# Attention's scratches split in two, its load pools opened with the prologue, and later layers' weights turned amid the prologue

## The chip, the cores and the metric

The kernel runs on one core of a Trainium2 chip, in one launch. The metric is the device time of one execution in microseconds, from runs without a profiler. A further execution was recorded by the hardware profiler; its times, counted from its first instruction, are those of the profile.

## The reference

The input is x (3327 tokens of 128 features) and a dense array adj (3327 by 3327, mostly zeros, but read in full). Four layers follow, each of the form layernorm(x + layer(x)). The first is an attention whose reshape makes it large:

```python
q = (x @ Wq.T).reshape(d, n, h)          # d = 128, n = 3327, h = 8
k = (x @ Wk.T).reshape(d, n, h)
v = (x @ Wv.T).reshape(d, n, h)
a = jnp.einsum('dnh,dmh->dnm', q, k) * scale
a = a + spatial_encoding + edge_encoding  # both are adj
a = jax.nn.softmax(a, axis=2)
out = jnp.einsum('dnm,dmh->dnh', a, v)
return out.reshape(n, h * d) @ Wo.T
```

So there are 128 "heads" of 3327 by 3327 scores over only 8 features each: 1.4 thousand million exponentials. Head d reads a flat stretch of the projected array, tokens 26 d to 26 d + 26 or so. The other three layers are products with adj or its transpose, with normalisations by its row or column sums, and small weights w1, w2 and w3.

## The kernel before

**Prologue** (the block with the pools pw, pa, ppw, pps). Tokens are taken in seven "supers" of 512 (the last has 255); `spread` says how they lie. At the start x of all supers is loaded (`xr`), transposed on TensorE and copied to `xT` (VectorE) and `xN` (ScalarE). The weights Wq, Wk and Wv are loaded and transposed by `load_by_h`. Then, for each super u:

- `split(u, wqT, q_s, ...)` multiplies 128 tokens at a time by Wq (`products`, two PSUM buffers pp), writes the high part `hi` on ScalarE and the rest `lo` on VectorE, reduces `hi` to a largest value (`top_q`) on VectorE, and stores both from GpSimd's queue to the DRAM scratch q_s (`store_slots`); `split` with Wk does the same for k_s. `hi` and `lo` have a tag of their own each, with two buffers.
- `values_projected(u)` makes `vp`, eight features of the values by 512 tokens.
- `values_turned(d)` turns the values of two heads on TensorE into `vo` (copied by VectorE and ScalarE in turn), for all heads whose tokens are there; after every 16 heads ScalarE issues four stores to the scratch v_img.
- For u from 1 to 4, 128 rows of adj are loaded (`ar`) and reduced to their largest values (`tops`). `ar` and `vo` share the tag "wide" of two buffers.

After the last super, the weights of later layers (w1, w3, Wo) are transposed and stored to DRAM, and a flag is computed that says whether queries and keys are small enough.

**Attention** (`attention`). Queries are taken in seven blocks of CW = 476 columns, keys in four blocks of 6 or 7 times 128, so there are 28 blocks. In each, 32 groups of four heads follow each other. `load_edges` loads a block of adj (`e_in`), which TensorE transposes into the PSUM of the scores. `load_heads` loads queries and keys of one group (`qt`, `kt`, 11 DMAs on SP's queue), two groups ahead; `load_values` loads a pair of groups' values (`vs`), which GpSimd copies into `v_pad`. `copy_queries` makes negated and copied rows of `qt` on VectorE. Then, per head, three sets of scores are multiplied, go through the exponential on ScalarE (one in 24 is computed on VectorE instead), and are multiplied by the values (`weigh`). Beside this, the background transposes adj to DRAM piece by piece (`piece_load` into `ai`, `piece_work`, `piece_store`).

**What sets the order.** In attention the order on TensorE, ScalarE, GpSimd and VectorE is written out by hand. SP's order, and all of the prologue, is laid out by a scheduler when the kernel is built. Each engine runs its instructions in order and waits at each for what it needs. Transfers signal eight semaphores for SP and ScalarE together and eight for GpSimd, in turn: a new transfer waits until the one eight before it has landed. A pool that lies on memory of a closed pool waits until all users of that are done. So the first loads of attention wait for the whole prologue.

Of the kernel before, what the change touches and what calls it, by code (L numbers as in the profile page):

```python
# [10 lines left out]
F32 = mybir.dt.float32  # L11
# [8 lines left out]
P = 128  # L20
GROUP = 4
# [29 lines left out]
def kernel(ctx: ExitStack, tc: tile.TileContext, x, adj, wq, wk, wv, wo,  # L51
# [62 lines left out]
    q_s = scratch.tile([2 * H, RS], F32, name="q_s")  # L114
    k_s = scratch.tile([2 * H, RS], F32, name="k_s")

    v_img = scratch.tile([P, T * HD], F32, name="v_img")
# [126 lines left out]

    with tc.tile_pool(name="pw", bufs=1) as pw, tc.tile_pool(name="pa", bufs=2) as pa, \
# [9 lines left out]
        xT = pw.tile([P, NU, 4, P], F32, name="xT")  # L255
        xN = pw.tile([P, NU * SUPER], F32, name="xN")
        wqT = load_by_h(pw, ppw, wq, "wqT")
        for u in range(NU):
            base, R, full, rest = spread(u)
            xr = pa.tile([P, 4, D], F32, name="xr")  # L260
# [11 lines left out]
            nc.vector.tensor_copy(xT[:, u, 0:R, :], ps[:, 0:R, :])  # L272
            nc.scalar.copy(xN[:, base:base + R * P].rearrange("c (p r) -> c r p", r=R), ps[:, 0:R, :])
            if u == 0:
                wkT = load_by_h(pw, ppw, wk, "wkT")
                wvT = load_by_h(pw, ppw, wv, "wvT")

        def store_slots(eng, dram, row, u, sb):

            base, R, full, rest = spread(u)  # L280
            width = dram.shape[1]
            for a, n, k in ([(0, P, R)] if full == P else [(0, 112, R), (112, full - 112, R), (full, 1, rest)]):
                eng.dma_start(out=flat_ap(dram, row * width + (base + R * a) * D, [[R * D, n], [width, H], [1, k * D]]),
                              in_=sb[a:a + n, :, 0:k, :].rearrange("p h r j -> p h (r j)"))

        def products(u, r, w):
            pp = pps.tile([P, HD], F32, tag="pp", name="pp")
            for c in range(0, HD, 512):
                nc.tensor.matmul(pp[:, c:c + 512], lhsT=xT[:, u, r, :], rhs=w[:, c:c + 512], start=True, stop=True)
# [13 lines left out]
        def values_projected(u):  # L303
            n = spread(u)[1] * P
            vp[u] = pa.tile([P, H, SUPER], F32, name="vp")
            for h in range(H):
                ps = pps.tile([P, SUPER], F32, tag="ps", bufs=3, name="pv")
                nc.tensor.matmul(ps[:, 0:n], lhsT=wvT[:, h * D:(h + 1) * D], rhs=xN[:, u * SUPER:u * SUPER + n],
# [3 lines left out]
        def values_turned(d):  # L312

            g, i = d // 16, d % 16
            if i == 0:
                vo[g] = pa.tile([P, 4, T, 32], F32, tag="wide", name="vo")
# [16 lines left out]
            if i == 14:  # L333
                for k0, nt in KBS:
                    w = nt * 32
                    nc.scalar.dma_start(out=flat_ap(v_img, k0 * HD + g * 4 * w, [[T * HD, P], [w, 4], [1, w]]),
                                        in_=vo[g][:, :, k0:k0 + nt, :].rearrange("p g s c -> p g (s c)"))

        def split(u, w, s, top, f):
            hi = pa.tile([P, H, 4, D], F32R, tag="hi", name="hi")  # L340
            lo = pa.tile([P, H, 4, D], F32R, tag="lo", name="lo")
# [15 lines left out]
        for u in range(NU):  # L357
            split(u, wqT, q_s, top_q, SCALE / 2)
# [6 lines left out]
            if 1 <= u <= 4:  # L365
                ar = pa.tile([P, NP], F32, tag="wide", name="ar")
                load_rows(nc.sync, ar[:, 0:N], adj, u - 1)
                nc.vector.tensor_reduce(tops[:, u - 1:u], ar[:, 0:N], AX.X, ALU.max)
            if u == 4:
                store_tops(pw, 0, tops, P)  # L370
        assert d == D

        w1T = load_transposed(pw, ppw, w1, "w1T")
        nc.gpsimd.dma_start(out=w1T_s, in_=w1T.rearrange("p a b -> p (a b)"))
        w3T = load_transposed(pw, ppw, w3, "w3T")
        nc.gpsimd.dma_start(out=w3T_s, in_=w3T.rearrange("p a b -> p (a b)"))

        wo_raw = pw.tile([P, HD], F32, tag="w_raw", name="wo_raw")
        nc.sync.dma_start(out=wo_raw, in_=wo)
        woT = pw.tile([P, HD], F32, name="woT")  # L380
        for h in range(H):
            ps = ppw.tile([P, P], F32, tag="w_ps", name="w_ps")
            nc.tensor.transpose(ps, wo_raw.rearrange("p (j h) -> p h j", h=H)[:, h, :], ident)
# [854 lines left out]
```

## Time and profile before

| what | us |
|---|---|
| median of 3 runs | 10949.95 (10942.28 to 10952.19) |
| the profiled execution's own time | 10954.31 |
| its span, first to last instruction | 10952.1 |
| ScalarE busy / TensorE busy in the span | 9867.2 / 10557.4 |
| first exponential of attention starts | 333.9 |
| last exponential starts | 10179.5 |

Busy TensorE is not TensorE at its peak, since matmuls overlap and their ends are modelled. In the profile L611 is the exponential, L603 the scores, L628 the product with the values, L596 the transposes of adj, L463 and L470 the loads of queries and keys, L437 and L439 those of e_in, L283 the stores of q_s and k_s, L289 the products of the prologue, L345 and L346 its hi and lo, L327 the turning of values and L336 their stores, L88 the load of ar.

### The profile page before, as it was taken

What the parts mean: (1) busy time and instruction counts of PE and PEld (TensorE: products, weight loads), DVE (VectorE), ACT (ScalarE), POOL (GpSimd) and SP (SyncE); (2) the same over time, 40 slices, a digit from 0 to 9 for tenths busy, and PEclk for the clock granted to TensorE, in tenths of its full rate; (3) what the DMA queues carried; (4) which work ended last, traced back from release to release, by engine and by line L of the source; (5) the groups of instructions that cost most, each with busy time, mean ns of one, the idle gap of its engine ahead of it and who ended that gap; (6) DMA issues with size and microseconds to landing.
All of it is one profiled execution on the core that took longest, in us unless ns stands there. A gap on an engine that the chain in (4) does not pass through costs nothing. (4 is left out here: it accounts for less than half of the span.)

```text
span 10952.1 us, 201583 instructions
## 1 busy us (share of the span) xinstructions
PE 10557.4 (96%) x76941; PEld 4117.7 (38%) x76941; DVE 7291.7 (67%) x8351; ACT 9867.2 (90%) x10783; POOL 1585.4 (14%) x2742
## 2 busy tenths in 40 slices
PE   8899999999999999999999999999999999999999
PEld 5333333333333333333333333333333333333779
DVE  6566776667776677766777667776677766667412
ACT  3799999999999999999999999999999999999400
POOL 0111122111221111211112111121111100001200
PEclk9899999999999999999999999999999999999999
DMA  7988888888888888888888888888888888888676
GB/s 251 155 127 122 128 133 132 127 123 129 134 132 128 123 127 132 135 123 127 128 132 134 120 122 120 123 132 125 127 127 123 120 119 116 115 112 117 207 284 244
DMA packets 995053, 1516.11 MB, mean 138 GB/s; under 512 B 202471, under 2 KB 812577, under 8 KB 980267
## 3 DMA queue, kind: packets, MB, share of 16 engines
q1 hardware_dynamic: 896854, 1371.75, 78.7%
q0 software_dynamic: 79616, 116.88, 4.6%
q8 instruction: 623, 10.21, 0.5%
q10 hardware_dynamic: 17620, 14.49, 0.4%
q14 instruction: 340, 2.79, 0.1%
HBM read 1371.86 MB, written 130.35 MB: 137 GB/s over the span
## 5 line engine op out<-in xcount | busy, mean ns | idle before, releaser
L611 ACT ACTIVATE e<-sc 128x952 f32<-128x952 f32 (+1 forms) x10304 | 9644.5, 1067 | 227.8 <-PE sc L603 219.9
L628 PE MATMUL o<-e,v_pad 128*32 128x476 f32 (+1 forms) x46592 | 5639.9, 573 | 39.9 <-DVE acc L641 36.7
L603 PE MATMUL sc<-qt,kt 64*128 64x476 f32 x23296 | 4474.9, 438 | 252.6 <-ACT e L611 167.3
L603 PEld LDWEIGHTS sc<-qt,kt 64*128 64x128 f32 x23296 | 2187.6, 184 | 4561.8 <-ACT e L611 4254.8
L628 PEld LDWEIGHTS o<-e,v_pad 128*32 128x32 f32 (+1 forms) x46592 | 1039.9, 108 | 1942.4 <-issue 1898.4
L509 POOL COPY v_pad<-vs 128x192 f32<-128x192 f32 (+1 forms) x896 | 441.6, 519 | 8127.9 <-DMA vs<-v_img 6389.5
L567 DVE TENSOR_SCALAR ey<-sc 128x952 f32<-128x952 f32 x448 | 515.0, 1150 | 1631.8 <-PE sc L603 1631.2
L573 DVE SCALAR_TENSOR_TENSOR e<-e,ey 128x952 f32<-128x952 f32 x1344 | 1546.0, 1150 | 43.2
L493 DVE TENSOR_SCALAR qt<-qt 32x1428 fp32r<-32x1428 f32 x896 | 801.8, 895 | 428.9 <-DMA qt<-q_s 347.7
L495 DVE CAST qt<-qt 64x1904 fp32r<-64x1904 f32 x896 | 1035.1, 1155 | 30.5
L234 POOL DMA_DIRECT2D adjT_s<-at x1352 | 796.2, 596 | 185.4 <-DMA adjT_s<-at 130.8
L569 DVE SCALAR_TENSOR_TENSOR ey<-et,ey 128x952 f32<-128x952 f32 x448 | 516.5, 1153 | 15.5
L573 DVE SCALAR_TENSOR_TENSOR e<-e,et 128x952 f32<-128x952 f32 x448 | 514.7, 1149 | 12.5
L573 DVE SCALAR_TENSOR_TENSOR e<-ey 128x952 f32<-128x952 f32 x448 | 515.2, 1150 | 0.0
L1074 PE MATMUL bank<-y,eT 128*128 128x128 f32 (+1 forms) x4056 | 473.9, 276 | 0.4 <-DVE h L1196 0.4
L1074 PEld LDWEIGHTS bank<-y,eT 128*128 128x128 f32 (+1 forms) x4056 | 465.3, 192 | 5.7 <-DVE h L1196 0.6
L641 DVE TENSOR_TENSOR acc<-o,acc 128x476 f32<-128x476 f32 x231 | 150.2, 650 | 422.6 <-PE o L628 422.0
L494 DVE TENSOR_SCALAR qt<-qt 32x476 fp32r<-32x476 f32 x896 | 357.0, 398 | 7.6 <-DMA qt<-lead_s 5.9
L568 DVE TENSOR_SCALAR et<-ey 128x952 f32<-128x952 f32 x448 | 296.9, 663 | 15.4
L570 DVE TENSOR_SCALAR et<-et 128x952 int32<-128x952 int32 x448 | 295.0, 659 | 15.4
L1034 ACT ACTIVATE rstd<-mv,eps 128x1 f32<-128x1 f32 x104 | 30.4, 292 | 265.1 <-DVE mv L1032 265.1
L648 POOL DMA_DIRECT2D o_s<-acc x308 | 191.5, 626 | 35.8 <-DVE acc L641 22.4
(152 smaller groups left out, 2404.6 us busy)
## 6 DMA issues: line engine op xcount, KB each, us to landing
kt<-k_s SPq DMA_DIRECT2D x5320, 96.0 KB
kt<-k_s SPq DMA_DIRECT2D x1764, 128.0 KB
eT<-adjT_s SPq DMA_DIRECT2D x78, 1664.0 KB
qt<-q_s SPq DMA_DIRECT2D x896, 119.0 KB
qt<-q_s SPq DMA_DIRECT2D x1792, 59.5 KB
vs<-v_img SPq DMA_DIRECT2D x224, 224.0 KB
adjT_s<-at POOLq DMA_DIRECT2D x1352, 32.0 KB, 5.2
vs<-v_img SPq DMA_DIRECT2D x224, 192.0 KB
```

Of the source, the lines that this page charges most:

```text
L234: nc.gpsimd.dma_start(out=flat_ap(adjT_s, (t * P + 32 * q) * NP + c * PIECE, [[NP, 32], [P, ns], [1, P]]), in_=at[32 * i:32 * i + 32].rear ...
L493: return [(0.9, None, lambda: nc.vector.tensor_scalar(qt[32:64, 1:], qf[0:32, 0:GROUP - 1], -1.0, None, ALU.mult)), (0.4, None, lambda: nc ...
L494: (0.4, None, lambda: nc.vector.tensor_scalar(qt[32:64, 0], before, -1.0, None, ALU.mult)),
L495: (1.2, None, lambda: nc.vector.tensor_copy(qt[64:128], qf[0:64]))]
L509: nc.gpsimd.tensor_copy(vp[:, 32:32 + nt * GROUP * 32].rearrange("p (x c) -> p x c", c=32)[:, :, 0:H], vs.rearrange("p (x c) -> p x c", c=H))
L567: nc.vector.tensor_scalar(y, x, -58 * math.log(2.0), 2 / math.log(2.0), ALU.max, ALU.mult)
L569: vec.append((1.2, of, lambda: nc.vector.scalar_tensor_tensor(y, t, ROUND, y, ALU.subtract, ALU.subtract)))
L573: vec.append((1.2, of, lambda i=i, a=a: nc.vector.scalar_tensor_tensor(e, e if i else y, a, t if i == len(POLY) - 1 else y, ALU.add, ALU.m ...
L603: nc.tensor.matmul(s[:, i, 0:CW], lhsT=kt[64 * rg:64 * rg + 64, k, pos * P:(pos + 1) * P], rhs=qt[64 * rg:64 * rg + 64, k, :], start=False ...
L611: nc.scalar.activation(e[:, 0:n, :], s[:, 0:n, 0:CW], AF.Exp, scale=2.0)
L628: nc.tensor.matmul(o[32 * j:32 * j + 32, 0:CW], lhsT=values[b, g][:m, c:c + 32], rhs=es[b, g * GROUP + j, r][:m, :], start=(r == 0 and u = ...
L1074: nc.tensor.matmul(ps[:n, 0:D], lhsT=e[:m, s, :n], rhs=y[:m, s, col:col + D], start=(s == 0), stop=(s == T - 1))
```

## The change

- q_s, k_s and v_img become two DRAM scratches each. Groups from LATE = 29 on (values: from VLATE = 28) read the second one, all others the first, to which the last super writes nothing. Tokens of super 5 that both need are stored to both.
- The pools kq (kt, qt, vs) and ed (e_in) are opened before the prologue's pools and stay open through attention.
- To make room, x is transposed super by super (`tokens_turned`) into double-buffered xT and xN; hi, lo and ar share a tag of three buffers; vo has a tag of its own and half the size, so v_img is stored after every 8 heads.
- The weights w1, w3 and Wo are turned after super 3 and no longer after the last.

In the order as built, SP issues e_in and the leading row of the keys at the start, the loads of groups 0, 1 and 2 between the loads of x and ar, and reads the flag among the first loads of attention. The last product with Wk (super 6) stands on ScalarE behind the last stores of v_img.

```diff
-    q_s = scratch.tile([2 * H, RS], F32, name="q_s")
-    k_s = scratch.tile([2 * H, RS], F32, name="k_s")
-    v_img = scratch.tile([P, T * HD], F32, name="v_img")
+    q_s = [scratch.tile([2 * H, RS], F32, name=f"q_s{i}") for i in range(2)]
+    k_s = [scratch.tile([2 * H, RS], F32, name=f"k_s{i}") for i in range(2)]
+    v_img = [scratch.tile([P, T * HD], F32, name=f"v_img{i}") for i in range(2)]
+    LATE, VLATE = 29, 28
...
+    early = ctx.enter_context(ExitStack())
+    kq = early.enter_context(tc.tile_pool(name="kq", bufs=3))
+    ed = early.enter_context(tc.tile_pool(name="ed", bufs=1))
...
-        for u in range(NU):
+        def tokens_turned(u):
             base, R, full, rest = spread(u)
+            xTs[u] = pa.tile([P, 4, P], F32, name="xT")
+            xNs[u] = pa.tile([P, SUPER], F32, name="xN")
             xr = pa.tile([P, 4, D], F32, name="xr")
...
-            for a, n, k in ([(0, P, R)] if full == P else [(0, 112, R), (112, full - 112, R), (full, 1, rest)]):
-                eng.dma_start(out=flat_ap(dram, row * width + (base + R * a) * D, [[R * D, n], [width, H], [1, k * D]]),
+            late = max(0, ((LATE * GROUP - 1) * N // D - base) // R)
+            parts = [(0, P, R)] if full == P else [(0, 112, R), (112, full - 112, R), (full, 1, rest)]
+            pieces = [(0, *x) for x in parts] if u < NU - 1 else []
+            pieces += [(1, *x) for x in parts] if late == 0 else [(1, late, P - late, R)] if late < P else []
+            for i, a, n, k in pieces:
+                eng.dma_start(out=flat_ap(dram[i], row * RS + (base + R * a) * D, [[R * D, n], [RS, H], [1, k * D]]),
...
-            g, i = d // 16, d % 16
+            g, i = d // 8, d % 8
             if i == 0:
-                vo[g] = pa.tile([P, 4, T, 32], F32, tag="wide", name="vo")
+                vo[g] = pa.tile([P, 2, T, 32], F32, name="vo")
...
-            hi = pa.tile([P, H, 4, D], F32R, tag="hi", name="hi")
-            lo = pa.tile([P, H, 4, D], F32R, tag="lo", name="lo")
+            hi = pa.tile([P, H, 4, D], F32R, tag="hl", bufs=3, name="hi")
+            lo = pa.tile([P, H, 4, D], F32R, tag="hl", bufs=3, name="lo")
...
+            if u:
+                tokens_turned(u)
             split(u, wqT, q_s, top_q, SCALE / 2)
...
-                ar = pa.tile([P, NP], F32, tag="wide", name="ar")
+                ar = pa.tile([P, H, 4, D], F32, tag="hl", bufs=3, name="ar").rearrange("p h r j -> p (h r j)")
...
+            if u == 3:
+                w1T = load_transposed(pw, ppw, w1, "w1T")
+                nc.gpsimd.dma_start(out=w1T_s, in_=w1T.rearrange("p a b -> p (a b)"))
+                w3T = load_transposed(pw, ppw, w3, "w3T")
...
+                nc.gpsimd.dma_start(out=woT_s, in_=woT)
             if u == 4:
                 store_tops(pw, 0, tops, P)
...
-        with tc.tile_pool(name="acc", bufs=1) as accp, tc.tile_pool(name="kq", bufs=3) as kq, \
-                tc.tile_pool(name="ed", bufs=1) as ed, tc.tile_pool(name="ex", bufs=1) as ex, \
+        with tc.tile_pool(name="acc", bufs=1) as accp, tc.tile_pool(name="ex", bufs=1) as ex, \
...
-                                      in_=flat_ap(q_s, a * RS + c0 + d * N, [[RS, n], [N, GROUP], [1, CW]]))
+                                      in_=flat_ap(q_s[g >= LATE], a * RS + c0 + d * N, [[RS, n], [N, GROUP], [1, CW]]))
...
     attention()
+    early.close()
```

The loads of kt and vs choose their scratch in the same way as that of qt. In the changed kernel the exponential is L629, hi and lo are L361 and L362, the stores of q_s and k_s L298, those of v_img L351.

## The prediction

> **What bounds the kernel now.** I read the page first. Its costliest group is the exponential on ScalarE:
>
> ```profile
> L611 ACT ACTIVATE e<-sc 128x952 f32<-128x952 f32 (+1 forms) x10304 | 9644.5, 1067 | 227.8 <-PE sc L603 219.9
> ```
>
> 9644.5 us of a 10952.1 us span go to it, so attention is bound by ScalarE. I then compared the built orders: from the first transposes of scores on, TensorE, VectorE, ScalarE and GpSimd run the same instructions in the same order in both kernels (only the three steps that set the flag move in among VectorE's first ones). So 9.8 of 10.95 ms have no reason to move; what counts is when the exponentials begin to run without gaps. Next the busy time of L611 by windows (window, length, ScalarE busy, clock, DMA share, GB/s):
>
> ```profile
> 333.90:379.70 45.80, 33.97 (x33) 0.76 0.95 139
> 379.70:425.50 45.80, 45.76 (x46) 1.00 0.87 120
> ```
>
> From 379.7 us on there are no gaps. Before it 33.97 us of exponentials were done, so the start is worth as much as one without gaps at 379.70 - 33.97 = 345.7 us. The timeline shows when the prologue let go:
>
> ```profile
> 304.83 3.07 ACTq L336 DMA_DIRECT2D v_img<-vo  x4
> 308.49 0.61 POOL L385 DMA_DIRECT2D woT_s<-woT  x1 [11.09 <-ACT woT L141]
> 311.88 0.38 SPq L437 DMA_DIRECT2D e_in<-in_adj_dram  x1
> 333.92 1.36 ACT L611 ACTIVATE e<-sc 128x1428 f32<-128x1428 f32 x1 [25.72 <-PE sc L603]
> ```
>
> e_in's load waits for all that the prologue has in flight, because its pool lies where the prologue's lay: 311.9 us is when the last transfer landed. Between 311.9 and 345.7, 33.8 us are lost. To what, the waits from 300 to 380 us say (total, times, longest):
>
> ```profile
> ACT e L611 <- PE sc L603: 37.6, 9, 25.7
> DVE qt L493 <- DMA qt<-q_s: 28.0, 3, 16.1
> PE sc L596 <- DMA e_in<-in_adj_dram: 18.0, 2, 12.3
> ```
>
> ScalarE starves for scores, TensorE for e_in, VectorE for queries: all of it is loads that start late. Last, the DMA of the prologue (0 to 310 us):
>
> ```profile
> q0 software_dynamic: 14096, 54.71, 52.6%
> q10 hardware_dynamic: 16457, 13.31, 13.3%
> q1 hardware_dynamic: 3124, 11.44, 10.7%
> q_s<-hi POOLq DMA_DIRECT2D x6, 2048.0 KB, 7.6
> ```
>
> The engines of the DMA are 76.7% taken, mostly by the stores of q_s and k_s; a store of hi lands 7.6 us after its issue (lo: 12.9). There is room for more, but not much.
>
> **What the Trainium skill says.** "DMA: Bandwidth & Descriptors", section "Anatomy of one DMA", says that a semaphore is waited for by the issuing sequencer, not by the DMA engines. So a load that waits on SP holds up every load behind it; the trace agrees (SP stood 64.4 us before L437 once). The same page, "Queues, rings and completion order": each engine of the DMA takes packets from the queues in turn. So early loads on SP share each engine with GpSimd's stores and lengthen their 7.6 us. No row of before shows these two together. "TensorE: Matmul & The Clock Gate", Part 1: TensorE drops to half clock after about 3.4 us of idling and takes as long to come back. The trace agrees: 0.50 from 310 to 330 us, 0.62 from 340 to 350.
>
> **The change, part by part.** Sums against this execution's 10954.3 us (span 10952.1 and 2.2 around it), which is 4.4 us above the median of the runs, 10949.95.
>
> 1. *Loads of attention before the prologue's end.* The pools kq and ed no longer lie on the prologue's memory. In the built order SP issues e_in at the start, the keys and queries of groups 0 and 1 once the stores of tokens 0 to 511 have landed, those of group 2 and both value pairs amid supers 2 and 3; the second e_in waits for TensorE's first transposes. Of the 33.8 us what stays: the first exponential still waits for all landings (its tile's pool reuses prologue memory), TensorE starts at half clock, and group 3's loads follow a 1.67 MB e_in. But group 3 is asked for at the end of group 0, as in the steady state, with two groups (about 25 us) to land. I leave 4 us (0 to 10): gain 33.8 - 4 = 29.8.
>
> 2. *Turning woT, w1T, w3T amid super 3.* The 11 transposes and 11 small copies are the same. At the tail the woT store went out at 308.5, but the last v_img store was only issued by 307.9. So this frees 0 to 4 us; I take 1. If its cover there (VectorE's and ScalarE's idling) were gone, 11 copies of 0.29 us are 3 us.
>
> 3. *One tag hl with 3 buffers for hi, lo and ar, in place of two hi, two lo and a shared "wide".* Each tile takes the buffer of the third before it: lo of k takes that of hi of q in the same super, whose store must have landed. It is issued about 1 us after the last hi of q and takes 7.6 us or more; VectorE meanwhile finishes lo (1.2), reduces hi (4.4) and copies vp (2 to 3 x 0.68). The store is there 8.6 us after the last hi, VectorE 7.0 to 7.6 us after it: nearly level, and lo is late when the store takes 10 to 13. Behind the waiting lo stand VectorE's copies of vo, and TensorE's next pp, which has two banks. I take 1.5 us in each of 6 supers: +9 (0 to +30).
>
> 4. *ar's reduce (3.62 us x 4) moves from amid lo to amid the turning of values*, where VectorE idled 45.1 us for TensorE (vo from vtr, 19 times). In the timeline at 111.4 us it stood right before the reduce that lo of k waited for. Up to -14; I take -8. Its load waits for the landing of lo of q and no longer for v_img stores (which held SP 141 us).
>
> 5. *Tokens turned per super.* The same 26 transposes and 14 copies, no longer in a burst from 5 to 25 us. Now each super has 4 x 0.27 on TensorE and 0.69 on VectorE ahead of its first product: 6 x 1.8 = 11, less what the start saves (at most 8). +3 (0 to +10). The loads of x on SP stand behind key loads that wait for stores of an earlier super, and two xr buffers are one super ahead: no stall, if SP runs on.
>
> 6. *v_img in 64 stores of half the size.* 32 more issues on ScalarE at 0.77 us (3.07 / 4): 24.6 us. While values are turned ScalarE idled 48.5 us for TensorE, which covers most. I take +6 (0 to +25). Against it, ScalarE was held 9.5 us at 215 and 12.2 us at 269 in such issues, with 1.7 MB of ar in flight: -9 (-15 to +5).
>
> 7. *More bytes in the prologue.* Three groups of 1.13 MB, 0.45 MB of values, 1.67 MB of e_in, 4 x 0.34 MB stored twice (tokens in both scratches, 4 issues of GpSimd more), less 0.5 MB of ai: 6.4 MB, 25 us at the prologue's 257 GB/s, 50 us at the 127 GB/s that such loads have in attention. Idle are 23.3% of 310, 72 us. If that cover were gone, all 25 to 50 us would show. I take +3 (0 to +25), because the loads are spread over four supers.
>
> 8. *The tail.* k of super 6 comes last on ScalarE and waits for the landing of lo of super 5; lo of 6 for that of hi of q. In before, 47.6 us passed from the store of lo of super 5 (264.3) to 311.9; counting the new chain by the same rows (turns and v_img issues 28, hi 2, reduce 2.3, lo 2.4, issues 1.5, landing 9) gives some 45. -2 (-10 to +15).
>
> The prologue: -1 + 9 - 8 + 3 + 6 - 9 + 3 - 2 = +1. The gain is 29.8 - 1 = 28.8, in the span 10923, in the median 10949.95 - 28.8 = **10921 us**.
>
> **Rivals.** *A: the prologue eats it.* The waits of part 3 and the traffic of part 7 come out near their upper ends, and the prologue ends 7 to 50 us later. For it: 76.7% of the DMA is taken already and 101% of it from 250 to 300 us. Against: these loads are small beside the 54.7 MB of stores. With +18: 10939.
>
> *B: slower, by SP standing in line.* A load of keys waits on SP for stores of k; behind it stand the loads of x for the next super, whose products fill those stores. If each of six supers starts 10 us late for that, the prologue is 60 us longer: 10949.95 - 29.8 + 60 = 10980. It turns to slower beyond (29.8 + 22) / 6 = 8.6 us a super. Against: xr of super u is issued once the tokens of super u - 2 are turned, some 40 us ahead. For: eight transfer semaphores now serve SP and ScalarE in turn, so a v_img issue too can wait for a load of SP.
>
> *C: the loads don't come early.* If reads of a scratch waited for all of its writers, groups 0 to 2 would start after super 5's stores, some 30 us before the end. Built, they wait for super 0's alone, so I give this little; it would still be about 10932. It counts with A.
>
> *D: more.* The v_img stalls vanish and ar is free: prologue 20 us shorter, 10900.
>
> **How the numbers follow.** A measurement of this kernel tells 0.2%, 22 us, from nothing. Forecast (gain 22 to 38) 0.47, D 0.11, A with C 0.30, B 0.12. Faster 0.58, same 0.30, slower 0.12. The unknown terms of the prologue reach from -43 to +110 if all went one way; together I take -28 to +39, which gives 10893 to 10960. The forecast's own range is 10912 to 10928.
>
> **What would show it.** Right: e_in and keys of groups 0 to 2 on SP before 250 us; first exponential within 2 us of the last landing; L611 without gaps within 10 us of its start; SP's wait before e_in gone. Part 3 shows as waits of L362 for q_s stores, part 6 as ScalarE's queue at L351, B as TensorE waiting for xr. Wrong would make me: a last landing after 330 us, or gaps in L611 past its first 15 us.

## The result, and the profile after

| | before | changed |
|---|---|---|
| median, 18 runs each, us | 10946.61 (10939.01 to 10953.98) | 10966.81 (10956.62 to 10974.84) |
| ratio | 1 | 1.0019 (1.0012 to 1.0025) |
| the profiled execution's own time and span | 10954.31, 10952.1 | 10974.84, 10973.1 |

The changed kernel is 20 us slower (0.19%), clear of the noise and just under the 0.2% that was set as the limit of "the same". The forecast was 10921, with a range that ended at 10960, so it was wrong in sign and outside its range.

The page of the changed kernel, costliest group, shows that attention itself did not change:

```profile
L629 ACT ACTIVATE e<-sc 128x952 f32<-128x952 f32 (+1 forms) x10304 | 9645.3, 1064 | 207.3 <-PE sc L621 198.6
```

9645.3 us of exponentials after, 9644.5 before. The difference lies ahead of them. SP's timeline of the changed kernel shows that the loads come early, as built (start, length, instruction; three of the lines):

```profile
3.05 0.42 SPq L455 DMA_DIRECT2D e_in<-in_adj_dram  x1
...
67.53 6.00 SPq L488 DMA_DIRECT2D kt<-k_s  x10
...
118.95 6.52 SPq L488 DMA_DIRECT2D kt<-k_s  x5
```

ScalarE's busy time in L629 by windows of the changed kernel (window, length, busy, clock, DMA share, GB/s), cut, as in the prediction, where the gaps end:

```profile
359.10:378.60 19.50, 16.44 (x16) 0.65 0.78 172
378.60:424.40 45.80, 45.72 (x46) 1.00 0.69 98
```

Only 3.1 us are lost between the first exponential (359.17) and the gapless run. Before, 33.8 us were lost after the last landing. But GpSimd's timeline of the changed kernel gives the last stores of the keys:

```profile
312.77 1.61 POOL L298 DMA_DIRECT2D k_s<-lo  x2
...
352.46 1.98 POOL L298 DMA_DIRECT2D k_s<-lo  x3 [2.90 <-DVE lo L362]
```

and that of the kernel before:

```profile
264.30 0.89 POOL L283 DMA_DIRECT2D k_s<-lo  x1
...
293.21 1.46 POOL L283 DMA_DIRECT2D k_s<-lo  x2
296.87 0.54 POOL L283 DMA_DIRECT2D k_s<-lo  x1 [2.20 <-DMA q_s<-lo]
```

The stores of the last super come in three pieces, and the first of them is issued 59.3 us later (352.46 in place of 293.21). All that the prologue sends has landed at about 358.5 us in place of 311.9: 46.6 us later. (358.5 is an estimate: the trace has no landing for the last piece, issued at 353.91; in runs 1 and 6 below that piece took 4.7 us.) The two differences are not the same because the order at the end changed: before, the last stores of v_img follow the keys (304.83, in the prediction); in the changed kernel they stand ahead of them. 46.6 less the 30.1 us gained in the transition is the 16.5 us by which the gapless run starts later; 3 to 4 us more are spread over attention.

Three measures are used for every run below. **Key store**: when the first piece of the last super's k_s<-lo is issued. **50th**: when the fiftieth exponential starts; it holds the prologue and the transition, and no more. (It is worked out within merged lines of the timeline; the single records lie up to 0.3 us later.) **Stretch u**: from the key store of super u - 1 to that of super u, for u from 1 to 6. All three are read from one execution of each kernel, and how well they repeat was not measured; two edits that changed next to nothing (runs 7 and 15) moved the key store by 0.9 and 0.3 us and the 50th by 0.7 and 0.4. The expectations call stretch 1 the "first super", stretch 5 the "sixth", stretch 6 the "last".

| stretch, us | 1 | 2 | 3 | 4 | 5 | 6 |
|---|---|---|---|---|---|---|
| before | 40.2 | 41.8 | 41.9 | 42.9 | 50.9 | 28.9 |
| changed | 47.9 | 52.5 | 49.3 | 50.6 | 66.4 | 39.7 |

Every stretch is 7 to 16 us longer, so it is nothing that happens once. Who waited for whom from 0 to 360 us, changed kernel (total, times, longest):

```profile
DVE lo L362 <- ACT hi L361: 58.2, 27, 4.9
...
DVE vo L146 <- DMA v_img<-vo: 39.6, 5, 11.9
...
ACT vo L144 <- DMA v_img<-vo: 35.8, 4, 12.4
...
DVE qt L512 <- DMA qt<-lead_s: 6.0, 1, 6.0
```

The two lines in the middle are new: before, copies of vo waited for TensorE's turns, for each other or for ScalarE's own queue, never for a store to land. With two buffers of eight heads a buffer comes round after four more pairs of heads, and the copy into it waits until the store out of it has landed. The prediction has no term for this. That gives theory V: these waits make the prologue longer. Rivals are H (the three buffers for hi, lo and ar do), T (the traffic of the early loads does) and K (the tokens turned by super do).

### The profile page after: what moved, and what is told of

Its sections match the earlier page's. It is cut to its first block, busy times and chain, and to the rows that moved or that the text cites. A ratio compares the mean times of both kernels' runs of the same rounds, so it can differ in the third digit from the quotient of the medians.

```text
span 10973.1 us, 201655 instructions
## 1 busy us (share of the span) xinstructions
PE 10566.2 (96%) x76941; PEld 4111.8 (37%) x76941; DVE 7292.6 (66%) x8351; ACT 9869.9 (90%) x10783; POOL 1596.0 (15%) x2746
## 5 line engine op out<-in xcount | busy, mean ns | idle before, releaser
L629 ACT ACTIVATE e<-sc 128x952 f32<-128x952 f32 (+1 forms) x10304 | 9645.3, 1064 | 207.3 <-PE sc L621 198.6
```

The source lines that it names most:

```text
L629: nc.scalar.activation(e[:, 0:n, :], s[:, 0:n, 0:CW], AF.Exp, scale=2.0)
```

## The experiments

All times are medians of 4 to 20 runs beside the kernel before on the same chip, whose median was 10946.6 to 10951.3 us. "to before" is the difference of the two medians; the other differences compare kernels through it. By the recorded ratio only runs 6, 9 and 17 reach 0.2%. In the prologue an edit also makes the scheduler lay out the order anew, so a run shows what an edit does together with its new order.

| run | time | to before | ratio, 95% interval | key store | 50th |
|---|---|---|---|---|---|
| before | | | | 293.2 | 395.8 |
| changed | 10966.81 | +20.2 | 1.0019 (1.0012 to 1.0025) | 352.5 | 411.9 |
| 1 four vo buffers | 10932.73 | -16.3 | 0.9983 (0.9977 to 0.9990) | 323.4 | 383.2 |
| 2 half values alone | 10940.38 | -8.6 | 0.9992 (0.9985 to 0.9999) | 275.2 | 380.6 |
| 3 three hl alone | 10931.99 | -17.0 | 0.9983 (0.9975 to 0.9992) | 280.0 | 374.5 |
| 4 tokens by super alone | 10959.47 | +10.5 | 1.0007 (0.9999 to 1.0016) | 305.0 | 408.3 |
| 5 tokens ahead | 10934.39 | -16.0 | 0.9986 (0.9979 to 0.9992) | 328.4 | 386.8 |
| 6 no early loads | 11011.41 | +61.0 | 1.0056 (1.0040 to 1.0073) | 349.9 | 436.2 |
| 7 weights at the end | 10969.17 | +18.8 | 1.0018 (1.0009 to 1.0026) | 351.6 | 411.2 |
| 8 row block apart | 10935.56 | -14.8 | 0.9989 (0.9982 to 0.9995) | 276.8 | 380.6 |
| 9 late, four hl | 10991.53 | +40.3 | 1.0037 (1.0023 to 1.0052) | 342.8 | 432.5 |
| 10 late, all buffers | 10952.95 | +1.7 | 1.0001 (0.9992 to 1.0010) | 313.0 | 402.9 |
| 11 group 0 early | 10934.59 | -16.7 | 0.9983 (0.9976 to 0.9990) | 315.3 | 389.0 |
| 12 the same, tokens first | 10933.06 | -18.2 | 0.9982 (0.9975 to 0.9990) | 305.7 | 380.0 |
| 13 one scratch | 10946.25 | -2.5 | 0.9999 (0.9990 to 1.0008) | 300.9 | 399.1 |
| 14 tokens first | 10939.91 | -8.9 | 0.9993 (0.9984 to 1.0002) | 300.1 | 392.3 |
| 15 full-size values | 10959.40 | +10.6 | 1.0011 (1.0002 to 1.0020) | 312.7 | 403.3 |
| 16 full values, group 0 | 10942.97 | -5.8 | 0.9994 (0.9985 to 1.0003) | 312.5 | 387.6 |
| 17 keys early only | 10927.03 | -21.1 | 0.9980 (0.9972 to 0.9988) | 307.4 | 378.3 |
| 18 one scratch, early pools | 10932.26 | -15.8 | 0.9986 (0.9979 to 0.9993) | 299.2 | 385.1 |

### 1. Four buffers for vo in the changed kernel

```diff
-                vo[g] = pa.tile([P, 2, T, 32], F32, name="vo")
+                vo[g] = pa.tile([P, 2, T, 32], F32, bufs=4, name="vo")
-        zero = pw.tile([4 * H, 512], F32, name="zero")
+        zero = pw.tile([4 * H, 512], F32, tag="woT", name="zero")
-        one = pw.tile([1, 512], F32, name="one")
+        one = pw.tile([1, 512], F32, tag="wqT", name="one")
```

> The changed kernel with four buffers for the turned values (vo) in place of two; room for them comes from putting the two constant tiles of the prologue's tail into buffers of weights that are done with. Measured by the last landing of the prologue (358.5 us in the changed kernel, 311.9 us before) and by the time. Theory V, that the copies into vo wait for the value stores to land because two half-size buffers come round every 5.8 us: those nine waits (75.3 us over two engines) vanish, the last landing comes 25 to 40 us earlier, at 318 to 334 us, and the time falls to about 10927 to 10942. Theory H, that the three shared buffers of hi and lo hold the queries and keys up: the last landing stays within 8 us of 358.5 and the time at 10959 or above. Theory T, that the traffic of the loads pulled ahead slows every landing: as theory H.

The key store comes 29.1 us earlier, the 50th 28.6, and the time falls by some 36 us. GpSimd's timeline with four buffers:

```profile
323.39 1.98 POOL L298 DMA_DIRECT2D k_s<-lo  x3 [2.91 <-DVE lo L362]
```

What the copies of vo waited for, in the changed kernel (us, times):

```profile
  DMA v_img<-vo: 75.3, 9
  PE vtr L342: 66.7, 33
```

and with four buffers:

```profile
  PE vtr L342: 77.8, 36
  DMA v_img<-vo: 13.4, 3
```

V is shown for the changed kernel: 29.0 of the 46.6 us by which its last landing is late (329.5 with four buffers). The two constant tiles that had to move for it are not the cause: run 10 below adds the buffers without them, and gains as much.

### 2, 3, 4 and 8. One part alone on the kernel before

Run 2 has the edits of `values_turned` only, run 3 those of the tag hl only, run 4 those of `tokens_turned` only. Run 8 has one line:

```diff
-                ar = pa.tile([P, NP], F32, tag="wide", name="ar")
+                ar = pa.tile([P, NP], F32, bufs=1, name="ar")
```

> The kernel before with one part of the change alone: turned values collected eight columns at a time, in two own buffers of half the size, and stored in 64 transfers of half the size. Theory V: the last landing goes from 311.9 to 337 us or later and the time up by 25 to 40 us. Theories H and T: the last landing stays within 8 us of 311.9 and the time within 8 us of before; what it rises by is the ScalarE time of the additional stores.

> The kernel before with one part of the change alone: hi, lo and the adjacency row block of the row maxima share three buffers in place of two for hi, two for lo and a share of the wide ones. Theory H: the last landing goes from 311.9 to 330 us or later, and the time up by 18 to 35 us. Theory V: no more than the 9 us of part 3 of the prediction, so a last landing at 313 to 321 us and a time up by 1 to 9 us.

> The kernel before with one part of the change alone: the tokens of a super loaded and turned just ahead of its queries, in place of all seven supers at the start. Theory K, that each super now begins with the load and the turn of its own tokens on TensorE's path: 2 to 4 us a super, last landing at 325 to 335 us, time up by 12 to 20 us. Theories V, H and T: the 3 us of part 5, last landing within 6 us of 311.9.

> The kernel before with one edit: the adjacency row block of the row maxima in a buffer of its own in place of one shared with the turned values. Theory S, that what the runs with half-size values alone and with shared hi and lo alone gained (15 and 21 us at the fiftieth exponential) is in both the same thing, the row block and the turned values no longer waiting for each other: the fiftieth exponential at 374 to 382 us and a time of 10926 to 10936. The prediction's part 4 (8 us): 386 to 390 us and 10938 to 10942. If the gains came from the smaller stores or from the sharing itself: within 3 us of 395.8.

V's expectation of run 2 and H's of run 3 fell, and in sign: both kernels are faster than before, 50th 15.2 and 21.3 us earlier. What both edits do, whatever else, is to take ar out of the buffers of vo. Run 8 does that alone and lands on the same 50th as run 2, 380.6; its time is 14.8 us below the kernel before. So theory S holds. Why, the tile view of ar in the kernel before says (40 to 300 us): its four reduces run amid supers 1 to 5, and each makes VectorE wait for its load,

```profile
L368 DVE TENSOR_REDUCE tops<-ar x4: 3618/3619/3620, 111.4 to 247.4; 128x1 f32<-128x3327 f32 x4
...
  DMA ar<-in_adj_dram: 9.9, 4
```

while lo, and with it TensorE's next products, stand behind. With a buffer of its own only two reduces fall into this window, the last at 63.1, where VectorE had time:

```profile
L368 DVE TENSOR_REDUCE tops<-ar x2: 3607/3614/3620, 38.2 to 63.1; 128x1 f32<-128x3327 f32 x2
```

In run 3 the four reduces still lie between 95.1 and 211.5, but they stand among the copies of vo and wait 1.0 us in all.

Run 2 still shows waits of vo for its stores (41.8 us on VectorE, 18.4 on ScalarE) and still ends with run 8 at the 50th: alone, that wait is hidden. In the changed kernel it costs 28.6 us; why, run 4 helps to see. TensorE's timeline in the kernel before, super 1:

```profile
48.77 1.02 PE L289 MATMUL pp<-wqT,xT 128*128 128x512 f32 x2
...
54.00 12.84 PE L327 MATMUL vtr<-vp,turn 128*128 128x208 f32 x70
```

and with tokens by super:

```profile
57.68 14.41 PE L330 MATMUL vtr<-vp,turn 128*128 128x208 f32 x70
71.93 0.60 PE L273 MATMUL xtr<-ident,xr 128*128 128x128 f32 x4
...
73.56 3.70 PE L292 MATMUL pp<-wqT,xT 128*128 128x512 f32 x8 [0.93 <-DVE xT L274]
```

The transposes of the tokens (xtr) take turns with the projected and turned values (pv, vtr) in one PSUM ring of three buffers. Turned by super, they stand in that ring behind all turns of the super before. The queries of super 1, which used to start before the value turns and fill their gaps, now start after them: stretch 1 takes 51.1 us in place of 40.2. The 50th comes 12.6 us later. Nearly all of the cost lies in this one stretch, 10.9 us; stretches 2 to 6 together take 1.1 us more than before (207.6 and 206.5); before too, the queries of super 2 start only at 99.44, when the value turns (84.78 to 99.59) are done. So it is not 2 to 4 us a super, as theory K had it. The measured time, +10.5, is a little under what theory K expected, and its interval just reaches no change.

Now the wait of vo can be followed on TensorE. In run 2 the tokens were turned at the start, and the queries of the next super come at once after the value turns:

```profile
98.91 4.58 PE L327 MATMUL vtr<-vp,turn 128*128 128x208 f32 x24 [1.41 <-ACT vo L141]
103.34 3.60 PE L289 MATMUL pp<-wqT,xT 128*128 128x512 f32 x8
```

In the changed kernel the tokens of the next super stand between the two. Their transposes wait for a place in the ring until a copy of vo is done, and the queries wait for the copy xT, which stands in VectorE's order behind copies of vo:

```profile
115.28 1.11 PE L281 MATMUL xtr<-ident,xr 128*128 128x128 f32 x4 [9.97 <-ACT vo L144]
...
166.42 6.34 PE L304 MATMUL pp<-wqT,xT 128*128 128x512 f32 x8 [7.81 <-DVE xT L282]
```

TensorE's waits for copies of vo (ahead of vtr and xtr) and for xT come to 35.8 us in the changed kernel, to 12.8 with four buffers (run 1), and to 10.0 in run 2. The first two differ by 23.0 us, most of what run 1 gains.

### 5. Tokens one super ahead, with four vo buffers

```diff
-            if u:
-                tokens_turned(u)
+            if u + 1 < NU:
+                tokens_turned(u + 1)
```

> The changed kernel with four vo buffers, and the tokens of a super turned one super ahead (ahead of the queries of the super before it), in two buffers as in the change. Measured by the start of the fiftieth exponential (395.8 us before, 411.9 in the changed kernel, 383.2 with four vo buffers alone). Theory K, that the turn of a super's tokens has its place in TensorE's order behind the value turns of the super before, so that no query product can fill the gaps of those turns: the fiftieth exponential comes 10 to 20 us earlier than with four vo buffers alone, at 363 to 373 us, and the time falls to 10912 to 10923. Rival, that the per-super tokens cost only the few us of their own turn: within 4 us of 383.

K's expectation failed. Stretch 1 fell from 47.8 to 42.7, but stretches 5 and 6 rose from 58.4 and 38.3 to 62.4 and 42.1, and the 50th is 3.6 us later. Placing the turn one super ahead doesn't give back what turning by super costs; why not is open.

### 6 and 7. Parts 1 and 2 undone in the changed kernel

Run 6 opens kq and ed in attention again; run 7 moves the block under `if u == 3` behind the last super.

> The changed kernel with part 1 alone undone: attention's pools of keys, queries and edges opened in attention again. Theory T, that the loads pulled ahead slow the prologue's own transfers: the last key store is issued 8 us or more earlier than in the changed kernel (352.5 us), and of the 30 us that the transition loses again less than 22 are left, so a time of 10975 to 10989. Rival, that the traffic costs the prologue nothing and part 1 is worth its 30 us: last key store within 3 us of 352.5, fiftieth exponential at 438 to 442, time 10993 to 11000.

> The changed kernel with part 2 alone undone: w1T, w3T and woT turned after the last super again. Theory W, that the weights amid super 3 hold up queries and keys: last key store 4 to 10 us earlier than 352.5, time 10956 to 10963. The prediction's part 2 (1 us): last key store within 3 us of 352.5, time within 4 us of the changed kernel, where the turns then lie after it and may add up to 5 us.

T falls: without early loads the key store is 2.5 us earlier, no more. From key store to 50th the early loads save 86.3 - 59.4 = 26.9 us. The time rises by more than that, some 41 us; 10 us of the rest are idle time of ScalarE ahead of the exponentials between 450 and 10150 us (201.4 in place of 191.5), for which I have no cause. The place of the weights makes no difference.

### 9 and 10. No early loads, and the buffers given back

Run 9 is run 6 with buffers of their own for hi, lo and ar. Run 10 adds `bufs=4` for vo.

```diff
-            hi = pa.tile([P, H, 4, D], F32R, tag="hl", bufs=3, name="hi")
-            lo = pa.tile([P, H, 4, D], F32R, tag="hl", bufs=3, name="lo")
+            hi = pa.tile([P, H, 4, D], F32R, tag="hi", bufs=2, name="hi")
+            lo = pa.tile([P, H, 4, D], F32R, tag="lo", bufs=2, name="lo")
```

> The changed kernel with part 1 undone (pools of keys, queries and edges opened in attention) and part 3 undone too: two buffers for hi, two for lo, one of its own for the adjacency row block; the values keep their two half-size buffers. To be read against the run without early loads (last key store issued at 349.9 us, fiftieth exponential at 436.2). Theory H, that the three shared buffers cost something beside the small vo buffers though they cost nothing alone: last key store 8 to 18 us earlier, at 332 to 342. Theory V alone: within 5 us of 349.9.

> The same, with four vo buffers as well, so that the prologue has every buffer back that attention's early pools took, but for the tokens turned by super. Theory B, that the prologue's growth of some 55 us is the buffers given up and nothing else but the 12 us that the tokens by super cost alone: the last key store at 285 to 298 us (the kernel before with the row block apart issued its first piece of it at 276.8, and the tokens by super add 12). If something else holds the prologue up (the stores into two scratches, the weights amid super 3): above 305 us.

Three buffers for hi, lo and ar cost 7.2 us at the key store and 3.7 at the 50th, between the two theories. vo's two cost 29.8 and 29.6 more, as in run 1. But B falls: with every buffer back the key store is at 313.0 and not below 298. Stretches 1 (52.8) and 6 (41.0) are long, where run 8 has 40.3 and 22.2.

### 11 and 12. All buffers, and only group 0 early

```diff
-    kq = early.enter_context(tc.tile_pool(name="kq", bufs=3))
+    kz = early.enter_context(tc.tile_pool(name="kz", bufs=1))
...
+        ... tc.tile_pool(name="kq", bufs=2) as kq, ...
-                kt = kq.tile([P, GROUP, 4 * P], F32R, name="kt")
+                kp = kq if (b * NHG + g) % 3 else kz
+                kt = kp.tile([P, GROUP, 4 * P], F32R, name="kt")
```

and qt in the same way. Run 12 has the tokens first, a ring `bufs=4` for hi, lo and ar, and three buffers for vo.

> The changed kernel with all of the prologue's buffers back and only the keys and queries of attention's first group and the edges loaded early: every third group keeps its keys and queries in a pool of one buffer that is opened with the prologue, the others rotate through two buffers opened in attention. Theory B: the last key store as in the run with all buffers and no early loads, within 5 us, and of the 30 us of the transition at most 10 lost again, because groups 1 and 2 load while group 0 computes; a time of 10895 to 10912. Rival, that groups 1 and 2 come too late: a second stall of 10 us or more after the first 12 exponentials, and a time of 10915 to 10930.

> As the run before it, with all tokens turned at the start as in the kernel before; room for them comes from a ring of four buffers for hi, lo and the row block, and three vo buffers. Theory K, that the tokens by super cost 12 us in this setting too: last key store and time 8 to 14 us earlier than in the run before it, a time of 10885 to 10902. If the ring and the third of vo's buffers eat that: within 4 us of it or later.

In run 11 the key store came as theory B said, but its rival was right on what follows (its time, 10934.6, lies above both ranges): after the first exponentials the others wait for groups 1 and 2 (run 11, ScalarE's timeline):

```profile
329.10 2.21 ACT L630 ACTIVATE e<-sc 128x1428 f32<-128x1428 f32 x2 [0.39 <-PE sc L622]
342.24 8.15 ACT L630 ACTIVATE e<-sc 128x952 f32<-128x952 f32 x8 [10.92 <-PE sc L622]
```

In run 12 the tokens gave 9.6 us at the key store and 9.0 at the 50th, but the time is the same within the intervals, not 8 to 14 us less.

### 13 to 15. What is left in run 10, one difference at a time

Run 13 has one scratch each for queries, keys and values, with the stores and loads of the kernel before. Run 14 turns all tokens at the start. Run 15 has vo for 16 heads in two buffers, and 32 stores.

> The run with all buffers and no early loads, with one scratch each for queries, keys and values in place of two. Read against that run (last key store issued at 313.0 us, last super 41.0 us, 10952.95 us). Theory Z, that the doubled stores of the sixth super and the traffic they make hold up the last one: last key store 10 to 18 us earlier, at 295 to 303. Theories K and N, that tokens or value stores do it: within 4 us of 313.

> The run with all buffers and no early loads, with all tokens turned at the start again. Theory K: the 12.5 us of the first super come back, last key store at 298 to 303, and the last super stays near 41 us; if the tokens also keep the last super's queries behind the values of the sixth, that comes down to 25 to 30 us too, and the last key store is at 282 to 290. Theories Z and N: no more than the first super's 12 us.

> The run with all buffers and no early loads, with the turned values in two buffers of full size and 32 stores as before, in place of four of half size and 64 stores. Theory N, that 64 stores keep ScalarE's queue (73.6 us of it over the prologue, where 32 took 40 to 47 us) and with it the copies that release TensorE: ScalarE's queue at 40 to 50 us and the last key store 8 to 15 us earlier, at 298 to 305. Theories Z and K: within 4 us of 313.

Z and K hold at the key store, with 12.1 and 12.9 us; N falls (0.3 us, though ScalarE's queue was held 49.2 us in place of 69.8, added up from the timelines; the 73.6 of the expectation is too high). Tokens first brings stretch 1 back to 39.0; one scratch brings stretch 6 from 41.0 to 27.1. In ScalarE's timeline of run 10 the four value stores after super 5 hold the queue for

```profile
276.22 7.46 ACTq L348 DMA_DIRECT2D v_img<-vo  x4
...
285.31 7.84 ACTq L348 DMA_DIRECT2D v_img<-vo  x4
```

right after GpSimd's doubled stores of super 5; with one scratch:

```profile
278.36 4.42 ACTq L345 DMA_DIRECT2D v_img<-vo  x4
284.42 4.24 ACTq L345 DMA_DIRECT2D v_img<-vo  x4
```

The doubled stores are what differs between the two kernels at that place; run 13 undoes the two scratches as a whole, so their other effects are in its numbers too. Yet of the 12.1 us only 3.8 are left at the 50th, and SP's first load after the prologue starts at 319.94 in place of 322.22: with the keys out of the way, the last value stores (308.00, 315.57) set the end. Part of the tokens' 12.9 stays: 10.6 at the 50th.

### 16 to 18. Versions that might beat both

Run 16 is the changed kernel with group 0 alone early, tokens first, and full-size values. Run 17 takes the early queries away:

```diff
-                qt = kp.tile([P, GROUP, CW], F32R, name="qt")
+                qt = kq.tile([P, GROUP, CW], F32R, name="qt", bufs=3)
```

Run 18 is run 3 with the pools kz and ed opened early and one scratch each.

> The changed kernel with early loads of the first group and the edges alone, all tokens turned at the start, the values in two buffers of full size with 32 stores, and the three shared buffers of hi, lo and the row block kept as in the change. It is the kernel before with the row block moved to hi and lo (10931.99 us, last key store at 280.0) plus early loads. If N and K hold: last key store at 280 to 290, first exponential within 12 us of it, time 10905 to 10918. If Z holds: last key store at 295 to 305, time 10918 to 10930.

> The run with full-size values and the first group early (last key store 312.5 us, sixth super 67.6 us, 10942.97 us), with the first group's queries in a buffer opened in attention, so that only keys and edges load early and no query copy stands in VectorE's order amid the prologue. Theory Q, that the early query copies hold VectorE up: the sixth super 10 to 18 us shorter, at 50 to 58 us, the last key store at 295 to 303, and the first exponential about 12 to 18 us after it because the queries load late; time within 8 us of 10943. If the stores and the three buffers do it: sixth super within 4 us of 67.6 and a time of 10945 or more.

> The kernel before with the row block in the shared hi and lo buffers (10931.99 us, last key store 280.0, first exponential 315.4) and two edits more: the pool of the edges and a one-buffer pool for the first group's keys and queries opened with the prologue; one scratch each as before. Edges load early; keys and queries of the first group wait for the last store into their scratch, but not for the prologue's pools to close. If that is enough for a good part of part 1's gain: first exponential 10 to 20 us earlier, at 295 to 306, and a time of 10912 to 10924, below both kernels. If the loads of the later groups just stall it afterwards: a time of 10926 to 10936.

Run 16 missed. Stretch 5 took 67.6 us, and VectorE's timeline says why:

```profile
242.16 0.68 DVE L146 COPY vp<-pv 128x512 f32<-128x512 f32 x1
253.49 0.40 DVE L508 TENSOR_SCALAR qt<-qt 32x476 fp32r<-32x476 f32 x1 [10.64 <-DMA qt<-lead_s]
253.92 1.15 DVE L509 CAST qt<-qt 64x1904 fp32r<-64x1904 f32 x1
255.09 1.23 DVE L359 SCALAR_TENSOR_TENSOR lo<-pp,hi 128x1024 fp32r<-128x1024 f32 x1
```

Attention's query copies stand in VectorE's order amid super 5. They wait 10.64 us for a load, and lo stands behind them, then TensorE's products (10.06 us), then hi (13.68 us). The load is that of the leading rows from lead_s, which GpSimd stores only after the row maxima of adj are done (232.45 and 233.61 in run 16), so it can't be early. Without early queries stretch 5 takes 57.7 us, 9.9 less: theory Q is shown, at the lower end of what it expected. (The key store came at 307.4, later than expected, and the time 16 us below run 16, more than expected, though the 50th moved by 9.3.) The changed kernel has the same wait, 6.0 us at 284.66. Run 17 has the lowest ratio of all, 0.9980 (0.9972 to 0.9988). Run 3, and run 8 with one line, are near it; their intervals overlap, so no order among them is shown. In run 18 the later groups stalled it, as its second branch said, but that is not all:

```profile
246.08 0.40 DVE L499 TENSOR_SCALAR qt<-qt 32x476 fp32r<-32x476 f32 x1 [7.48 <-DMA qt<-lead_s]
...
337.98 8.15 ACT L616 ACTIVATE e<-sc 128x952 f32<-128x952 f32 x8 [17.99 <-PE sc L608]
```

The early query copies hold VectorE here too, 7.48 us. Its key store is 19.2 us later than that of run 3, and its first exponential, at 314.1, is only 1.3 us earlier than run 3's. How much of the 19.2 us this wait makes is open.

## Why the prediction was wrong

**Part 1** was right at its place: 30.1 us measured in the transition, 29.8 predicted (by its own trace the store of woT lands at 312.8, so 311.9 is the last landing that e_in waits for, not the last of all); run 6 without it loses 26.9 from key store to 50th. It left out what else moves with a load: the query copies that follow it on VectorE (6.0 us of waiting in the changed kernel, 9.9 us of stretch 5 in run 17). Its remark on the clock is only in part what the trace shows. In steps of 2 us TensorE's clock in the kernel before is at half from about 308, some 2 us after the last matmul of the prologue, and full again at 340, some 6 us after the scores began to follow each other closely; then it falls to half once more from 344 to 352, with TensorE busy 1.5 to 2.0 us of every 2. The 0.62 is this second fall, and the 3.4 us of the page aren't measured here.

**Part 2** was right: nothing (0.7 us at the 50th).

**Part 3**, +9 (0 to +30): alone the shared buffers cost nothing (run 3 is 6 us ahead of run 8 at the 50th, its time the same within the intervals), in company 3.7 to 7.2 us. The size was fair, but by luck: the wait named for it, lo for a landing store of q, is seen twice in run 3, with 3.7 us together, and not at all in the changed kernel.

**Part 4**, -8: the mechanism was right and the term too small; ar away from vo is worth 15.2 us at the 50th (run 8), more than the -14 given as its end. In the changed kernel the four reduces wait for their loads 0.4 us in all, in place of 9.9.

**Part 5**, +3, failed in its mechanism. It counted the transposes and copies, not their place: 12.6 us alone, 10.6 in company, nearly all of it in stretch 1, where the queries now stand behind the value turns. The range ended at +10. It also hands the wait of part 6 on to TensorE: the transposes and xT stand behind copies of vo. Run 5, which gives the tokens an earlier place, won nothing by it, so this account is not complete.

**Part 6**, -3 net, is the step that failed most. It priced 64 issues and took 9 us of queue stalls off; the stalls stayed (46.6 us of ScalarE's queue went to these stores before, 60.7 in the changed kernel, added up from the timelines). And it put at nothing, without a reason, the wait of the copies into a half-size buffer for the store out of it to land: 28.6 us at the 50th (run 1), nearly as large as the whole gain of part 1.

**Part 7**, +3: 2.5 us, right. The stores of hi of k land 12.8 us after their issue in place of 7.8, but most of that is not the early loads: without them it is 11.0, with hi, lo and ar in buffers of their own as well as four of vo 8.3. The Trainium skill says in "DMA: Bandwidth & Descriptors", "Queues, rings and completion order", that engines take packets from the queues in turn. No run here shows the turns themselves; what the early loads add to the landing of these stores is 1.8 us.

**Part 8**, -2, was right by its own count: from the store of lo of super 5 to the last landing it expected some 45 us in place of 47.6, and 312.77 to 358.5 is 45.7. What no part timed is the doubled stores of super 5, which part 7 counts as bytes alone: 12.1 us at the key store, 3.8 at the 50th (run 13).

The sum, at the key store, from runs that undo one thing each: -16.4 (row block, run 8) + 12.9 (tokens, run 14) + 29.1 (vo, run 1) + 7.2 (hi and lo, run 9) + 12.1 (scratches, run 13) + 2.5 (early loads, run 6) = +47.4, of 59.3 measured. At the last landing, taken in kernels without early loads from SP's first load of e_in, the same runs give -16.5 + 14.4 + 29.0 + 3.9 + 2.3 + 2.0 = +35.1, of 46.6. The effects aren't additive (vo's wait is hidden alone), and the missing 11 to 12 us have no place of their own; they stay open.

**Rival A** was what happened, and its own formula gives the measured time: 10949.95 - 30.1 + 46.6 = 10966. But that is luck as to the cause: neither of the two it named, the waits of part 3 and the traffic of part 7, came out near its upper end. Its top of 50 us was in the text, and +18 was chosen. **Rival B** did not happen: SP's waits ahead of the loads of x (L274) hold no query product up; TensorE's xtr waits for copies of vo (10.0 us), not for xr.

Of the marks given, the loads before 250 us and the first exponential within 2 us of the last landing were seen. The exponentials ran without gaps only 19.5 us after the first one, not within 10. Both marks that were to make it wrong came: "a last landing after 330 us", and gaps past the first 15 us, of 1.41 us ahead of 376.06 and 0.41 ahead of 378.68, which cost little.

That the vo wait shows in the changed kernel and hides in run 2 because of the tokens turned by super is read from the waits and orders of these traces: no run has tokens by super and half-size values alone.

## What to carry to other kernels

When a change makes room by shrinking buffers, ask of each how long it takes to come round and how long its store takes to land, and what the engines have to do meanwhile; here two buffers fewer cost nearly as much (28.6 us) as the early loads that they made room for had gained (30.1). A load moved ahead can take with it the instructions that use it, and in an engine's fixed order these hold up all that stands behind (9.9 us in run 17). Try each part of a large change alone: one line of this one, the row block in a buffer of its own, makes the kernel faster by 0.11% (0.05 to 0.18%).

## What the runs showed that I had not expected

The same attention, with the same exponentials in the same order, idled between 176.5 us (run 14) and 201.4 us (run 6) ahead of them from 450 to 10150 us, and 189.7 in the kernel before. I have no cause for it. Each figure is from one execution, and the times of one kernel alone differ by 15 us (the kernel before, 10939.0 to 10954.0), so much of it may be nothing that the edits make. An earlier end of the prologue need not show in one total time, then; the 50th exponential leaves this part out. Four issues of value stores on ScalarE's queue took from 1.96 to 9.54 us with stores of half size, and from 2.50 to 13.57 us with stores of full size. The edit of run 13 alone took one such group from 7.46 to 4.42 us, so what else is in flight matters.
